# Reordering VectorE and GpSimd work in a conditioned block with Strassen-type products: sums, one normalised tile, statistics, a gather

## The chip, the cores and the metric

The kernel runs on one core of a Trainium2 chip. Its engines each run their own queue of instructions in order: TensorE (PE; its weight loads are listed apart as PEld), VectorE (DVE), ScalarE (ACT), GpSimd (POOL) and SyncE (SP), which issues most DMAs. They wait for one another by semaphores. The metric is device time in microseconds (us): the median of three runs before the change is 456.7 us (455.54 to 456.86).

## The reference

Thirty-two sequences of 128 tokens with 512 features pass through a conditioned block. `t` is one row of conditioning for each sequence, `m` the mask of tokens.

```
emb = silu(t) @ ada_w + ada_b;  shift, scale, gate = split(emb, 3)
norm = where(m, layernorm(x) * (1 + scale) + shift, 0)
ssm  = gelu(norm @ ssm_w1 + b1) @ ssm_w2 + b2  (+ the same with bwd weights)
x    = x + gate * where(m, ssm, 0)
ff   = silu(t) @ ffada_w + ffada_b;  shift2, scale2, gate2 = split(ff, 3)
n2   = layernorm(x) * (1 + scale2) + shift2
h    = gelu(n2 @ ff_w1 + ff_b1)            # 512 -> 1024
out  = x + gate2 * (h @ ff_w2 + ff_b2)     # 1024 -> 512
```

All is float32. In the first half only tokens that the mask keeps are computed. The second half, from `ff` on, is dense over all 4096 tokens and takes most of the time.

## The kernel before

**Opening** (to about 83 us): conditioning rows, the first half on 512 gathered slots of tokens, whose rows go to `x1_rows` in DRAM, and sums of the weights of the feed-forward layer, kept in `t_rows` in DRAM.

**Pairs.** The second half goes in four pairs `p` of two sides; a side is four sequences. For every pair there are two products, each done with seven multiplications of quarter blocks in place of eight (Strassen's scheme in the form with few additions).

*First product* (class `FirstProduct`, L1024): `h` of a pair. It is cut twice: seven *streams* of the outer scheme, in the order 1, 2, 5, 6, 3, 7, 4 (`STREAMS`, L1015), and in each stream seven multiplications P1 to P7. One multiplication is a *phase* (`phase`, L1108), which writes one of the two PSUM banks `e` and `a` of its stream and then starts what the result needs. `window(new, old, fill)` (L1206) interleaves two streams:

```
(new, "P5"), (new, "P1"), (old, "P3"), (old, "P7"),
(new, "P2"), (new, "P6"), (old, "P4"),
```

After phase `n` of window `w` it runs the functions put at `(w, n)` by `put`. The steps that matter here, with their lines:

- `token_sums(j, n)` (L1036): DVE sums of quarters of the tokens, for `j` = 1 to 4 and four blocks `n`: L1046 (into `sx`, read by stream 5), L1050 (into `xn_sy`, read by stream 6), L1053 and L1056 (in place, for streams 7 and 4). Both inputs lie in SBUF. Pair 0 calls them at L1406 to L1426; later pairs inside the windows, their first ones at the end of the pair before.
- `seed` (L1157): once P1 is in `a`, it goes to `e`, on DVE with an earlier result added (L1161; streams 2, 6, 3, 7, 4) or on ACT (L1163). P2 then adds to `e` on PE, so PE waits for the seed.
- P6: DVE L1142 puts `a` plus an earlier sum into `e`; P3 adds to `e` and waits for it. P7: DVE L1147 takes `a` out into `hb`; P4 adds to `a` and waits for it. P4: L1152.
- `with_p5` (L1165, POOL L1168), `after` (POOL L1197) and `late_sum` (POOL L1201) are POOL's sums of 128x512, all in SBUF. `late_gelu` and `release` start ACT's gelu (L1079).

*Second product* (class `SecondProduct`, L1225): steps in `ORDER` (L902), "P1U P5U P1V P5V ...", U and V being two units of columns. `first_block` (DVE L1251) sums parts of `hb` into `s1`, which P5 reads; `seed` (L1239) starts its banks from `fb2` and `fb2_step` on ACT (L1243); L1261, L1268, L1278, L1280, L1326, L1328 and L1334 are its other DVE sums. The end of the first product is woven into it: stream 4's P3, P7 and P4 run between its first steps.

*The next pair's tokens.* `take_first_half` (POOL L885) gathers rows of the first half from `x1_rows` with an indirect DMA, one for each sequence, eight for each pair. `Statistics` (L904) has `one(i)` (DVE bn_stats and its aggregate, L917 and L918) for each tile, and `root` (DVE L922 `ve`, then POOL L923 `rstd`) for a side. `blocks(side, i)` normalises tile `i` (DVE L929) and transposes its 32x32 blocks (L1479). `to_feature_rows` issues 16 DMAs for a side from SP (L956), ACT scales what lands (L939), and `TokenBlocks.one` (L986) makes the sums that the next pair's first phases read. In pair 0 `fw2_of.combine` (L394) also makes sums of the second weights.

**What sets the order.** Everything from the opening on stands in a region of manual scheduling: each engine's queue is in the order in which the Python code issues the instructions. A wait of one instruction holds all behind it on its engine. The DVE queue before, around the first pair's start, is: `sx` blocks 0 and 1, stream 1's P6 (L1142), stream 2's seed, stream 1's P7 (L1147), `sx` blocks 2 and 3, stream 2's P6, the four `xn_sy` blocks, L1053 block 0, `fb2_step`, L1053 block 1, stream 2's P7 (L1147), and so on.

Of the kernel before, what the change touches and what calls it, by code (L numbers as in the profile page):

```python
# [14 lines left out]
ALU = mybir.AluOpType  # L15
# [7 lines left out]
def kernel(  # L23
# [49 lines left out]
    nc = tc.nc  # L73
    B, S, D = x.shape
    P = 128
    assert S == P
    G = 4
# [99 lines left out]
    def group_of_tiles(name):  # L177
        return xnp.tile([P, G, D], F32, tag="xn", name=f"xn_{name}")
# [398 lines left out]
    for key, vec in (("ssm1", ssm_b1), ("bwd1", bwd_b1), ("ff1", ff_b1)):  # L577
        n = vec.shape[0] // P
# [78 lines left out]
    fb2 = const.tile([P, D], F32, name="fb2")  # L657
# [177 lines left out]
    def in_turned_blocks(t):  # L835
        return t.rearrange("p i d -> p (i d)").rearrange("p (k i c) -> p k i c", i=G, c=P)
# [37 lines left out]
    fb2_step = const.tile([P, D // 2], F32, name="fb2_step")  # L874
# [7 lines left out]
    def take_first_half(p, xs, which=range(2 * G)):  # L882
        for i in which:
            b = 2 * p * G + i
            nc.gpsimd.indirect_dma_start(  # L885
                out=xs[i // G][i % G // 2][:, i % 2],
                out_offset=None,
                in_=x1_rows,
                in_offset=bass.IndirectOffsetOnAxis(ap=slot_i[:, b : b + 1], axis=0),
                bounds_check=NS - 1,  # L890
                oob_is_err=False,
            )
# [71 lines left out]
    def new_xT(p, side):  # L964
        return xtp.tile([P, KC, G * S], F32, tag=f"xT{side}", name=f"xT_{p}_{side}")
# [436 lines left out]
    now = FirstProduct(0, of_x[0].cut(), of_w)  # L1402
    now.load_weights(1)
    x_of[1][1] = load_side(1, 1)
    now.load_weights(2)
    for n in range(2):  # L1406
        now.token_sums(1, n)
    now.apart(1)
    now.do(1, "P1")
    now.seed(1)  # L1410
    now.do(2, "P1")
    now.do(1, "P5", "P2", "P6")
    now.do(2, "P5")
    now.seed(2)
    now.do(1, "P3")
    now.with_p5(2, "12")
    now.do(1, "P7")
    now.with_p5(2, "22")
    take_first_half(1, x_of[1], range(G))
    for n in range(2, 4):  # L1420
        now.token_sums(1, n)
    now.do(2, "P2", "P6")
    for n in range(4):
        now.token_sums(2, n)
    now.do(1, "P4")
    now.token_sums(3, 0)  # L1426
    for p in range(NP):
        more_pairs = p + 1 < NP
        xs = x_of[p]
        fills = {}  # L1430

        def put(w, n, f, *args):
            fills.setdefault(w, {}).setdefault(n, []).append(lambda: f(*args))

        if p:
            for n, at in enumerate(((1, 3), (1, 4), (1, 6))):
                put(*at, now.token_sums, 2, 1 + n)
            put(1, 6, now.token_sums, 3, 0)
        for n, at in enumerate(((2, 1), (2, 3), (2, 3))):
            put(*at, now.token_sums, 3, 1 + n)  # L1440
        for n, at in enumerate(((2, 4), (2, 4), (2, 6), (2, 6) if more_pairs else (3, 1))):
            put(*at, now.token_sums, 4, n)
        put(3, 6, now.load_weights, 3)
        if p == 0:
            put(3, 6, load_rows_of_fw2, 0)
            put(6, 2, fw2_of.combine, 0)
            put(6, 5, fw2_of.combine, 1)
        put(4, 6, now.load_weights, 4)
        if p == 0:
            put(4, 6, load_rows_of_fw2, 1)  # L1450
        second = SecondProduct(p, now.h, xs)
        if p == 0:
            put(
                2, 0, nc.vector.tensor_tensor,
                fb2_step, fb2[:, D // 2 :], fb2[:, : D // 2], ALU.subtract,
            )
        put(6, 0, now.late_gelu, "11")
        put(6, 1, second.seed, 0)
        put(6, 3, second.first_block, 0, 0, 2)
        put(6, 6, second.first_block, 0, 2, 4)  # L1460
        put(5, 4, now.late_sum, "11")
        put(6, 4, now.late_gelu, "12")
        put(6, 5, now.late_gelu, "22")
        put(6, 6, now.late_sum, "21")
        if more_pairs:
            x_next = x_of[p + 1]
            stats = [Statistics(x_next[side], f"{p + 1}_{side}") for side in range(2)]
            xn, xT = {}, {}

            def blocks(side, i):  # L1470

                if i == 0:
                    xn[side] = in_turned_blocks(
                        group_of_tiles(f"{p + 1}_0")
                        if side == 0
                        else sp.tile([P, G, D], F32, tag="s12", name=f"xn_{p + 1}_1")
                    )
                t = stats[side].normalised(i, xn[side][:, :, i])
                nc.vector.transpose(t, t)  # L1479

            def to_feature_rows(side, *queues):
                xT[side] = new_xT(p + 1, side)
                turned(xn[side], xT[side], queues)

            if p:
                put(1, 6, take_first_half, p + 1, x_next, range(G))
            put(2, 6, take_first_half, p + 1, x_next, range(G, G + 2))
            put(3, 4, take_first_half, p + 1, x_next, range(G + 2, G + 3))
            put(5, 4, take_first_half, p + 1, x_next, range(G + 3, 2 * G))
            for i, at in enumerate(((3, 1), (3, 3), (3, 4), (3, 6))):  # L1490
                put(*at, stats[0].one, i)
            put(*((3, 6) if p else (5, 4)), stats[0].root)
            for i, at in enumerate(((4, 4), (4, 6), (5, 3), (6, 4))):
                put(*at, stats[1].one, i)
            put(6, 4, stats[1].root)
        for w in range(1 + (p == 0), 7):
            now.window(STREAMS[w], STREAMS[w - 1], fills.get(w, {}))
        second.load_gate(0)
        second.step(0)
        now.late_gelu("21")  # L1500
        if more_pairs:
            for i in range(2):
                blocks(0, i)
        now.do(4, "P3")
        second.seed(1)
        now.do(4, "P7")
        second.first_block(1, 2, 4)
        if more_pairs:
            blocks(0, 2)
        second.step(1, late=True)  # L1510
        now.do(4, "P4")
        if more_pairs:
            blocks(0, 3)
            to_feature_rows(0, nc.sync)
        second.load_gate(1)
        second.first_block(1, 0, 2)
        second.seed_and_second_block(0)
        fill = {5: [lambda: second.third_block(0)], 7: [lambda: second.third_block(1)]}

        def put(step, f, *args):  # L1520
            fill.setdefault(step, []).append(lambda: f(*args))

        if p == 0:
            put(2, fw2_of.combine, 2)
            put(6, fw2_of.combine, 3)
        if more_pairs:

            for i in range(G):
                put(2 + i // 2, blocks, 1, i)
            for k in range(KC):  # L1530
                put(4 + k // 2, lambda k: scaled(2 * (p + 1), xT[0], k), k)
                put(7 + k // 2, lambda k: scaled(2 * (p + 1) + 1, xT[1], k), k)
                if k == 1:
                    put(4, to_feature_rows, 1, nc.sync, nc.sync, nc.sync, nc.scalar)

            def begin(j):
                if j == 1:
                    of_x[p + 1] = TokenBlocks(p + 1, (xT[0], xT[1]))
                of_x[p + 1].one(j)

            put(8, begin, 1)
            put(9, begin, 2)
            put(9, begin, 3)
            put(10, begin, 4)

            def next_product():
                nxt["p"] = FirstProduct(p + 1, of_x[p + 1].cut(), of_w)
                nxt["p"].load_weights(1)

            nxt = {}  # L1550
            put(10, next_product)
            put(11, lambda: nxt["p"].do(1, "P5", "P1"))
            for n in range(4):
                put(11 + n // 2, lambda n: nxt["p"].token_sums(1, n), n)
            put(13, lambda: nxt["p"].token_sums(2, 0))
            if p + 2 < NP:
                x_of[p + 2] = [[], []]
                put(11, lambda: x_of[p + 2][0].extend(load_side(p + 2, 0)))
            put(12, lambda: nxt["p"].do(1, "P2", "P6"))
            put(13, lambda: nxt["p"].load_weights(2))  # L1560
            if p + 2 < NP:
                put(13, lambda: x_of[p + 2][1].extend(load_side(p + 2, 1)))
        for step in range(2, len(ORDER)):
            second.step(step)
            for f in fill.get(step, ()):
                f()
        if more_pairs:
            now = nxt["p"]
# [11 lines left out]
    with tc.If(more > 0):  # L1580
# [11 lines left out]
        with tc.For_i(0, more, 1):  # L1592
# [12 lines left out]
            for half_no, (mod, was, wbs, bias, bcol, func) in enumerate(  # L1605
# [7 lines left out]
                for j, w in enumerate(was):  # L1613
                    n = FF // len(was)
                    nc.sync.dma_start(wa[:, :, ts(j, n)], w.rearrange("(k p) f -> p k f", p=P))
                for j, w in enumerate(wbs):
                    n = HC // len(wbs)
# [73 lines left out]
```

## Time and profile before

One execution was profiled. Its own time is 455.45 us, of which the span from first to last instruction is 453.7 us.

| what | value |
|---|---|
| median of three runs | 456.7 us |
| profiled execution, time / span | 455.45 / 453.7 us |
| mean granted clock of PE | 0.999 |
| busy: PE / DVE / ACT / POOL | 446.6 / 331.7 / 178.0 / 159.8 us |
| share of the last chain: PE / DVE | 92% / 5% |
| instructions: PE / DVE / ACT / POOL | 2151 / 571 / 390 / 154 |
| first product of pair 0 begins; pairs 1, 2, 3 begin | 83.4; 169.4, 260.4, 351.3 us |

A row of a timeline gives the start and the length in us, the engine, the line, the operation, the tile written and the tiles read (numbers of buffers left out), the shape, and how many records were joined. In brackets stands the idle time of the engine ahead of the row and what ended it. A row's length on DVE includes the fill and drain of its pipe: two rows that follow each other directly start 0.60 us apart at 128x512 though each is listed with 0.68. A row with PE's weight loads (PEld) stands 0.22 us ahead of its matmuls as long as PE is not held up.

### The profile page before, as it was taken

How to read it: one execution, taken by the hardware profiler on the slowest of the kernel's cores; microseconds unless marked ns; L12 is line 12 of the kernel's file. 1: busy time of each engine (PE TensorE's matmuls, PEld its weight loads, DVE VectorE, ACT ScalarE, POOL GpSimd, SP SyncE). 2: the span in 40 equal slices, each digit the busy share in tenths (PEclk: the TensorE clock that was granted, in tenths of full speed). 3: DMA queues.
4: the chain of work that ended last, by engine and by line, in shares of the span. 5: the costliest groups of instructions: out<-in, count | busy, mean ns of one | idle time of the engine just before them, and what ended most of it. 6: DMA issues, size and time to landing. Idle time of an engine off the chain costs nothing.

```text
span 453.7 us, 6170 instructions
## 1 busy us (share of the span) xinstructions
PE 446.6 (98%) x2151; PEld 370.4 (82%) x2151; DVE 331.7 (73%) x571; ACT 178.0 (39%) x390; POOL 159.8 (35%) x154
## 2 busy tenths in 40 slices
PE   8999999999999999999999999999999999999996
PEld 3884585688888888888888888888888888888885
DVE  5798797697789759886796498867963995534645
ACT  3124127244642552446425514454355154552000
POOL 4220550089770000797700007977000027560000
PEclk9999999999999999999999999999999999999999
DMA  7999449745518817722187167221872442222023
GB/s 251 379 396 407 150 73 326 279 151 172 189 78 180 114 49 251 249 92 82 66 191 107 56 230 264 95 84 54 202 105 59 157 145 82 81 94 93 0 82 107
DMA packets 82611, 70.57 MB, mean 156 GB/s; under 512 B 63112, under 2 KB 63728, under 8 KB 81554
## 3 DMA queue, kind: packets, MB, share of 16 engines
q1 hardware_dynamic: 67762, 58.28, 40.9%
q0 software_dynamic: 4160, 10.54, 6.9%
q10 hardware_dynamic: 10656, 1.33, 2.1%
q8 instruction: 18, 0.29, 0.2%
q14 instruction: 15, 0.12, 0.1%
HBM read 56.46 MB, written 13.70 MB: 155 GB/s over the span
## 4 chain that ended last, share of the span: by engine, by line
PE 92%; DVE 5%; POOL 1%; issue 1%; ACT 1%; DVEq 0%
PE a_o L1304 23%; PE a_m L1117 18%; PE e_o L1304 18%; PE e_m L1117 14%; PE po_s L221 6%; PE ph_s L204 5%; PE ph_s L673 2%; PE pm_ss L309 1%; PE last L1304 1%; PE pm_f L309 1%; PE a_m_alone L1117 1%; PE pl_s L254 1%; DVE xn_sy L1050 0%; PE part_s L333 0%; DVE e_m L1142 0%
## 5 line engine op out<-in xcount | busy, mean ns | idle before, releaser
L1168 POOL TENSOR_TENSOR ha<-p_m,ha 128x512 f32<-128x512 f32 x20 | 25.8, 1289 | 178.8 <-ACT ha L1175 169.2
L1304 PE MATMUL e_o<-fw,ha 128*128 128x256 f32 x256 | 57.9, 379 | 0.0
L939 ACT ACTIVATE xT<-xT,modT 128x128 f32<-128x128 f32 x112 | 44.1, 480 | 31.6 <-DMA xT<-xn 31.4
L1304 PE MATMUL a_o<-t,hb 128*128 128x256 f32 x240 | 54.1, 379 | 0.0
L1304 PEld LDWEIGHTS e_o<-fw,ha 128*128 128x128 f32 x256 | 48.6, 190 | 6.6
L1304 PEld LDWEIGHTS a_o<-t,hb 128*128 128x128 f32 x240 | 45.6, 190 | 6.2
L1079 ACT ACTIVATE hb<-hb,biasT 128x256 f32<-128x256 f32 x64 | 29.0, 500 | 30.4 <-POOL hb L1201 19.8
L1131 ACT COPY p_m<-e_m 128x512 f32<-128x512 f32 x27 | 15.8, 586 | 47.8 <-PE e_m L1117 43.3
L885 POOL DMA_INDIRECT x<-x_rows,slot_i x24 | 29.2, 1218 | 6.0 <-issue 5.3
L1168 POOL TENSOR_TENSOR hb<-p_m,hb 128x512 f32<-128x512 f32 x20 | 29.6, 1481 | 0.3
L1304 PE MATMUL a_o<-fw,ha 128*128 128x256 f32 x128 | 28.9, 379 | 0.0
L1304 PE MATMUL a_o<-t,s 128*128 128x256 f32 x128 | 28.9, 379 | 0.0
L1304 PE MATMUL e_o<-fw,s 128*128 128x256 f32 x128 | 28.9, 379 | 0.0
L221 PE MATMUL po_s<-w,h_s 128*128 128x512 f32 x64 | 28.4, 594 | 0.0
L1175 ACT COPY ha<-e_m 128x512 f32<-128x512 f32 x32 | 18.5, 578 | 24.9 <-PE e_m L1117 24.6
L1304 PEld LDWEIGHTS a_o<-t,s 128*128 128x128 f32 x128 | 24.3, 190 | 3.3
L1304 PEld LDWEIGHTS a_o<-fw,ha 128*128 128x128 f32 x128 | 24.3, 190 | 3.3
L1304 PEld LDWEIGHTS e_o<-fw,s 128*128 128x128 f32 x128 | 24.3, 190 | 3.3
L1142 DVE TENSOR_TENSOR e_m<-a_m,ha 128x512 f32<-128x512 f32 x20 | 13.9, 696 | 17.0 <-POOL ha L1168 6.6
L1079 ACT ACTIVATE ha<-e_m,biasT 128x256 f32<-128x256 f32 x48 | 20.0, 468 | 14.8 <-PE e_m L1117 12.6
L1117 PE MATMUL a_m<-xT,tw 128*128 128x256 f32 x96 | 24.7, 380 | 0.4 <-DVE hb L1147 0.4
L1117 PE MATMUL e_m<-s,fw 128*128 128x256 f32 x92 | 23.8, 381 | 0.0
(237 smaller groups left out, 892.3 us busy)
## 6 DMA issues: line engine op xcount, KB each, us to landing
tw<-t_rows SPq DMA_DIRECT2D x16, 896.0 KB, 5.3
x<-in_x_dram SPq DMA_DIRECT2D x16, 512.0 KB, 8.8
gate<-gate_rows POOLq DMA_DIRECT2D x8, 1024.0 KB, 5.2
out_dram<-x SPq DMA_DIRECT2D x15, 512.0 KB, 4.9
xT<-xn SPq DMA_DIRECT2D x92, 64.0 KB, 2.4
ada_f<-in_L_cond_ffada_w_dram SPq DMA_DIRECT2D x4, 768.0 KB, 13.2
ada_a<-in_L_cond_ada_w_dram SPq DMA_DIRECT2D x4, 512.0 KB
w<-in_L_cond_ssm_w_dram SPq DMA_DIRECT2D x2, 1024.0 KB, 6.2
```

The lines of the kernel that those rows point to most:

```text
L204: nc.tensor.matmul(ph[:, :n], w[:, k, ts(f, P)], xT[:, k, :], start=(k == 0), stop=(k == KC - 1))
L221: nc.tensor.matmul(po, h[f][:, ts(i, P)], w[:, f, :], start=(f == 0 and seeded is None), stop=(f == HC - 1), skip_group_check=seeded is no ...
L309: nc.tensor.matmul(pm[ts(j, B), : (hi - lo) * P], sT[:, k, :], kinds[:, k, lo:hi, ts(j, P)], start=False, stop=True, skip_group_check=True,)
L885: nc.gpsimd.indirect_dma_start(out=xs[i // G][i % G // 2][:, i % 2], out_offset=None, in_=x1_rows, in_offset=bass.IndirectOffsetOnAxis(ap= ...
L939: nc.scalar.activation(out, src, AF.Identity, bias=shift, scale=scale)
L1079: nc.scalar.activation(dst[:, n], src[:, n], AF.Gelu_apprx_tanh, bias=biasT[:, f : f + 1])
L1117: nc.tensor.matmul(bank[:, ts(n, QT)], self.w_block(j, product)[:, ts(n, P)], self.x_block(j, product), start=(product in ("P1", "P5") and ...
L1131: nc.scalar.copy(p5, e)
L1142: nc.vector.tensor_tensor(e, a, p5, add)
L1168: nc.gpsimd.tensor_tensor(self.place(RESULT[j], c), self.p5[j], other, ALU.add)
L1175: nc.scalar.copy(self.place(RESULT[j], c), src)
L1304: nc.tensor.matmul(part, src[:, k, ts(i, P)], w[product][:, k, :], start=(last and k == 0), stop=True, skip_group_check=True,)
```

## The change

Only the places in the order move; no instruction is added, removed or changed in shape. PE, ACT and SP issue the same instructions in the same order as before.

- Pair 0: all four `sx` blocks and then `fb2_step` stand ahead of stream 1's P6. `xn_sy` block 0 stands between stream 1's P6 and stream 2's seed, block 1 between that seed and stream 1's P7; blocks 2 and 3 stay behind stream 2's P6. On POOL the seventh gather (first row of tile `x_14`) moves from behind stream 6's three sums to ahead of them.
- All pairs: of side 0's statistics, `one(3)` moves from the end of window 3 to window 4 behind stream 3's seed, and from pair 1 on `root` with it (POOL's `rstd` then stands behind stream 3's two L1168 sums). Of side 1's, `one(1)` moves behind stream 7's seed. The root of side 1 moves behind `first_block(0, 2, 4)` on DVE and behind the last L1201 on POOL.
- Pair 0: the second tile to be normalised (`blocks(0, 1)`) moves behind stream 4's P7 (L1147).
- From pair 1 on: `xn_sy` block 0 (a sum for stream 6) moves from the end of the pair before to window 1, behind stream 2's seed.

```diff
-    for n in range(2):
+    for n in range(4):
         now.token_sums(1, n)
+    nc.vector.tensor_tensor(fb2_step, fb2[:, D // 2 :], fb2[:, : D // 2], ALU.subtract)
     now.apart(1)
     now.do(1, "P1")
     now.seed(1)
     now.do(2, "P1")
     now.do(1, "P5", "P2", "P6")
+    now.token_sums(2, 0)
     now.do(2, "P5")
     now.seed(2)
+    now.token_sums(2, 1)
     now.do(1, "P3")
     now.with_p5(2, "12")
     now.do(1, "P7")
     now.with_p5(2, "22")
     take_first_half(1, x_of[1], range(G))
+    now.do(2, "P2", "P6")
     for n in range(2, 4):
-        now.token_sums(1, n)
-    now.do(2, "P2", "P6")
-    for n in range(4):
         now.token_sums(2, n)
     now.do(1, "P4")
...
         if p:
-            for n, at in enumerate(((1, 3), (1, 4), (1, 6))):
-                put(*at, now.token_sums, 2, 1 + n)
+            for n, at in enumerate(((1, 1), (1, 3), (1, 4), (1, 6))):
+                put(*at, now.token_sums, 2, n)
...
-        if p == 0:
-            put(
-                2, 0, nc.vector.tensor_tensor,
-                fb2_step, fb2[:, D // 2 :], fb2[:, : D // 2], ALU.subtract,
-            )
...
-            put(2, 6, take_first_half, p + 1, x_next, range(G, G + 2))
-            put(3, 4, take_first_half, p + 1, x_next, range(G + 2, G + 3))
+            put(2, 6, take_first_half, p + 1, x_next, range(G, G + 2 + (p == 0)))
+            if p:
+                put(3, 4, take_first_half, p + 1, x_next, range(G + 2, G + 3))
             put(5, 4, take_first_half, p + 1, x_next, range(G + 3, 2 * G))
-            for i, at in enumerate(((3, 1), (3, 3), (3, 4), (3, 6))):
+            for i, at in enumerate(((3, 1), (3, 3), (3, 4), (4, 1))):
                 put(*at, stats[0].one, i)
-            put(*((3, 6) if p else (5, 4)), stats[0].root)
-            for i, at in enumerate(((4, 4), (4, 6), (5, 3), (6, 4))):
+            put(*((4, 1) if p else (5, 4)), stats[0].root)
+            for i, at in enumerate(((4, 4), (5, 1), (5, 3), (6, 4))):
                 put(*at, stats[1].one, i)
-            put(6, 4, stats[1].root)
+            put(6, 6, stats[1].root)
...
         if more_pairs:
-            for i in range(2):
+            for i in range(1 + (p > 0)):
                 blocks(0, i)
         now.do(4, "P3")
         second.seed(1)
         now.do(4, "P7")
+        if more_pairs and p == 0:
+            blocks(0, 1)
         second.first_block(1, 2, 4)
...
-            put(13, lambda: nxt["p"].token_sums(2, 0))
```

## The prediction

> **What bounds the kernel now.** I read the share of busy time and the chain first, then TensorE's (PE's) rows in order of time, then VectorE's (DVE's) and GpSimd's (POOL's) rows around every place where PE is late. From the page:
>
> ```profile
> PE 446.6 (98%) x2151; PEld 370.4 (82%) x2151; DVE 331.7 (73%) x571; ACT 178.0 (39%) x390; POOL 159.8 (35%) x154
> PE 92%; DVE 5%; POOL 1%; issue 1%; ACT 1%; DVEq 0%
> ```
>
> PE is the bound; only its gaps can be won. A phase is four matmul records, 0.864 us from its start to the next one's; sixteen are 3.455. PE's timeline (start, length) shows the exceptions:
>
> ```profile
> 97.75 1.03 PE L1117 MATMUL a_m<-sx,tw 128*128 128x256 f32 x4
> 99.00 1.13 PE L1117 MATMUL a_m<-xT,t 128*128 128x256 f32 x4 [0.23 <-DVE hb L1147]
> 99.97 1.03 PE L1117 MATMUL e_m<-xn_sy,tw 128*128 128x256 f32 x4
> ...
> 129.89 3.62 PE L1304 MATMUL e_o<-fw,s 128*128 128x256 f32 x16
> 133.93 1.13 PE L1117 MATMUL a_m<-xT,tw 128*128 128x256 f32 x4 [0.42 <-DVE hb L1147]
> ...
> 207.63 1.13 PE L1117 MATMUL e_m<-xT,tw 128*128 128x256 f32 x4
> ...
> 365.35 1.13 PE L1117 MATMUL e_m<-xT,fw 128*128 128x256 f32 x4
> ```
>
> From 97.75 to 99.00 is 1.25, so 0.39 is lost, and the phase after takes 0.97, another 0.10 that follows each such stop. In this way: stream 2 P4 (99.00) 0.49; stream 5 P3 (101.75) 0.16; stream 6 P2 (103.88) 0.41; stream 4 P4 (133.93) 0.69; stream 7 P2 in pairs 1 and 2 (207.63, 298.58) 0.28 each; stream 2 P2 in pair 3 (365.35) 0.29. Together 2.60 us. All wait for DVE, which is in other work. Outside these places, two more before 90 us and the start and end, PE's rows stand shoulder to shoulder.
>
> Why DVE is late, from its timeline and POOL's:
>
> ```profile
> 92.58 1.48 DVE L1046 TENSOR_TENSOR sx<-s 128x256 f32<-128x256 f32 x1
> ...
> 131.28 1.27 DVE L929 TENSOR_SCALAR xn<-x,mv,rstd 128x512 f32<-128x512 f32 x1
> ...
> 137.37 0.65 DVE L1251 TENSOR_TENSOR s<-hb 128x512 f32<-128x512 f32 x1
> ...
> 201.58 0.69 DVE L1147 TENSOR_TENSOR hb<-a_m,hb 128x512 f32<-128x512 f32 x1 [0.93 <-PE a_m L1117]
> ...
> 216.19 0.30 DVE L922 TENSOR_SCALAR ve<-mv 128x4 f32<-128x4 f32 x1
> ```
>
> ```profile
> 92.08 1.71 POOL L1168 TENSOR_TENSOR hb<-p_m,hb 128x512 f32<-128x512 f32 x1
> ...
> 98.59 1.00 POOL L885 DMA_INDIRECT x<-x_rows,slot_i  x1 [0.31 <-issue]
> 99.89 2.07 POOL L885 DMA_INDIRECT x<-x_rows,slot_i  x1 [0.30 <-issue]
> ...
> 131.00 1.26 POOL L1201 TENSOR_TENSOR hb<-hb 128x512 f32<-128x512 f32 x1
> ...
> 215.17 1.29 POOL L1201 TENSOR_TENSOR ha<-ha 128x512 f32<-128x512 f32 x1 [2.77 <-ACT ha L1175]
> ```
>
> A DVE sum of two SBUF tiles costs 0.41 (256 wide) or 0.68 alone, but 1.48 at 92.58: it ends 0.27 after POOL's 92.08 sum does (93.79). The normalised tile takes 1.27 in place of 0.53 and ends 0.29 after POOL's 131.00. The small ve takes 0.30 at 216.19 and ends at 216.49, POOL's at 216.46; without POOL such a tile takes 0.17. So these operations and POOL's sums take turns, one whole instruction at a time. Sums that read PSUM (L1142, L1147, L1152, L1161) and bn_stats keep 0.6 to 0.7 beside POOL.
>
> **The change part by part** (PE, ACT and SP keep their order; only DVE's and POOL's change).
>
> *First pair's sums.* Sums (1,2), (1,3) and fb2_step (0.60 + 0.34 + 0.34 from start to start) move to 86.15, where DVE idles 2.02 until 88.25: they end at 87.43. fb is issued at 77.4; with the 8.8 of other x loads it lands by 86.9, with 2.4 (the shortest kind) by 80.5: in time at both ends. Block (2,0) goes into the 0.71 idle before 89.66, (2,1) into the 0.68 before 91.04. So the pair 91.65 to 93.99 vanishes, 2.34 with its contention, and stream 2's P7 result (L1147) starts when PE allows, 96.02 + 1.13 (that lag stands in pair 1, 188.42 to 189.55) = 97.15, not 98.27. From there DVE has the sequence that it has in pair 1, where stream 6's seed starts 4.94 after that L1147 (194.49) and PE is never late. Gain: 0.49 + 0.16 + 0.41 = 1.06, all of it.
>
> *The seventh gather* now stands ahead of stream 6's sums on POOL; what queues behind it is L1168 twice, L1197, and through it stream 3's seed on DVE. POOL's sum ends at 93.4 (no contention), then seven gathers of at least 1.00 with 0.30 between: 102.7 if nothing disturbs; the six of before took 2.63 more in all, those of pair 1 1.23. DVE's sequence is now pair 1's, so I take 1.23: 103.9; ends 102.7 and 105.4. The Trainium skill ("SBUF — State Buffer", Who interferes with whom) says that a two-input DVE sum contends only with a GpSimd instruction that reads SBUF, not with one that only writes; read so, a gather's descriptors should not suffer, and 102.7 would be the time. The 2.07 row beside plain sums stands against that reading, and I do not use it. Stream 3's seed needs POOL three sums later (3.73), 107.6; PE frees it at 106.39 (107.44 less the gain) + 1.16 (as 107.44 to 108.60) = 107.55; the seed takes 0.76 with its signal, and PE's weight load is due at 108.76 (110.03 less 1.05, loads running 0.22 ahead). Slack 0.4: cost 0, up to 1.0 at the late end.
>
> *Statistics behind seeds.* In pairs 1 and 2 stream 7's seed goes ahead of bn_stats: at 206.07 instead of 206.89, so 0.28 per pair is won, with the 0.03 stop at 205.69. The bn_stats fall into DVE's idle 0.68 (209.92). But ve of side 0 now stands after stream 3's seed (199.95) and a bn_stats: 201.5. POOL, no longer in the root, runs L1168 twice from 200.06 to 202.55, and ve waits for the second: 202.58. Behind it stands L1147 of stream 6 P7 (201.58 before): 202.55 to 203.24, so PE's P4 starts at 203.30, not 203.11: 0.19 + 0.10 lost. Net per pair 0.31 − 0.29 = +0.02. If ve is not held, +0.31; ends −0.1 and +0.31. I take the held one, because three ve beside POOL sums end 0.03 after them.
>
> *One normalised tile, and the second root.* In pair 0, tile 1 moves behind stream 4's L1147, so P4 no longer waits 0.69. What is late next is unit V's P5 of the second product at 138.35: it needs L1251 (137.37 to 138.02), due for the weight load at 138.13. PE has no more than 0.05 there. DVE has no idle time from 126.19 (which follows PE through ACT and POOL, so 125.14 now) to 137.37. After L1251 (129.02 at its end) 6.57 of work is left (7.30 less the 0.73 of the tile's wait). ve stands there now; POOL's last sum, no longer behind the root, takes its turn at 129.09 and ends at 130.25, so ve and all behind it start at 130.25. L1251 then starts at 130.25 + 6.57 = 136.82, ends 137.47, PE follows at 137.53 instead of 138.35: 0.82 less 0.10 for the stop. So pair 0 keeps 0.72 of 1.06 + 0.69 = 1.75, as DVE sets that point. Ends: 0.72 − 0.25 if one more POOL operation comes between; 1.75 if DVE gets its turn first. In pairs 1 and 2 ve does the same, and L1201 runs ahead of the root: the wait of 0.84 at 224.50 goes, tile 0 waits about as long again; L1147 ends near 224.9, when the weight load is due (224.94). Cost 0 to 0.1.
>
> *Pair 3.* Stream 2's seed goes ahead of one sum (0.60): 0.29 won; if pair 2's tiles are 0.34 later, 0.2. I take 0.25.
>
> Sum: 0.72 + 0.02 + 0.02 + 0.25 = 1.0 us. The profiled execution took 455.45 (span 453.7), so 454.45; it lies 1.25 under the median of the runs, 456.7, so 455.7 for a median. About 0.3% (1.37 us) is what a measurement of this kernel can tell from no change.
>
> **The rivals.**
> *Everything comes through* (faster): DVE is not held where I hold it, and all 2.60 plus the two 0.03 are won: 454.1. For it: the waits named are exactly those that the order removes. Against it: the 1.27 and 1.48 rows, and 0.05 of slack at 138.13.
> *GpSimd becomes late*: seven gathers at the old mean, (104.09 − 93.94) / 6 = 1.69 each, end at 105.4; stream 3's seed starts at 109.1, PE gets it at 109.9 instead of 108.98: 0.9 + 0.10. The gain is gone: 456.7. It decides from 104.3 on. Against: pair 1's mean is 1.46.
> *The tiles are held in every pair* (slower): ve waits for L1168, tile 0 for L1201, tile 1 for the root, 1.2 + 1.26 + 1.05 in place of the 0.96 of before. Tile 1 is then 2.6 late; L1147 of stream 4 P4 has 1.23 of slack (223.65 + 0.06 to 224.94), so PE loses 1.4 + 0.10 in pairs 1 and 2, and pair 3's gain goes with the later transposes: −3.0 + 0.7 = 2.3 slower, 459.0. It decides from tile 1 being 1.2 late on. Against: the root beside tile 0 at 130.07 left it at 0.53.
>
> **How the numbers follow.** Forecast 0.42, everything 0.34, GpSimd late 0.13, tiles held 0.11. The forecast's own range, by its ends, is 454.8 to 456.6, and a third of it (0.14) lies more than 0.3% under 456.7. Faster 0.34 + 0.14 = 0.48; slower 0.10 of the last; the rest 0.42. The range 453.9 to 457.1 takes in the first three cases with their ends and leaves out the last.
>
> **What would show it.** Right: no stop of PE from 97 to 108 and at stream 4 P4 (or under 0.2), a stop of 0.6 to 0.9 at unit V's P5 in pair 0, one of 0.2 to 0.3 at stream 6 P4 in pairs 1 and 2, ve at 1.0 us or more there, seven gathers ending near 103.9. Wrong: PE tight at those P5 and P4 rows (ve short), or a wait of stream 3's seed for L1197, or DVE's tiles over 1.2 in pairs 1 and 2 with PE waiting for them.

## The result, and the profile after

The changed kernel takes 454.84 us (median of 13 runs, 453.79 to 455.84) beside 456.02 us for the kernel before (13 runs, 455.04 to 456.87). The ratio is 0.9971, its 95% interval 0.9959 to 0.9982: 1.18 us less by the medians, about 0.3%. The forecast was 1.0 us less. The interval spans 0.8 to 1.9 us, so which terms of the forecast came true is read from PE's stops below, not from the times.

The profiled execution of the changed kernel took 454.99 us with a span of 453.3 us, so one execution against one other shows 0.46 us only. The page has the same bound as before:

```profile
PE 446.3 (98%) x2151; PEld 370.5 (82%) x2151; DVE 334.2 (74%) x571; ACT 178.4 (39%) x390; POOL 159.0 (35%) x154
...
PE 94%; DVE 3%; POOL 1%; ACT 1%; issue 1%
```

DVE's share of the chain that ended last went from 5% to 3%, and its busy time rose by 2.5 us with the same instructions, since a held instruction counts as busy: the six rows of ve take 4.3 us more in all, those of L1046 1.4 less. PE's timeline of the changed kernel at the places shown before, and where new stops came:

```profile
97.80 1.03 PE L1117 MATMUL a_m<-sx,tw 128*128 128x256 f32 x4
98.67 1.03 PE L1117 MATMUL a_m<-xT,t 128*128 128x256 f32 x4
99.53 1.03 PE L1117 MATMUL e_m<-xn_sy,tw 128*128 128x256 f32 x4
...
132.34 1.03 PE L1117 MATMUL a_m<-xT,tw 128*128 128x256 f32 x4
133.20 3.62 PE L1304 MATMUL a_o<-fw,ha 128*128 128x256 f32 x16
137.44 3.72 PE L1304 MATMUL e_o<-fw,s 128*128 128x256 f32 x16 [0.62 <-DVE s L1251]
...
202.44 1.13 PE L1117 MATMUL a_m<-xn_sy,tw 128*128 128x256 f32 x4
...
293.38 1.13 PE L1117 MATMUL a_m<-xn_sy,tw 128*128 128x256 f32 x4
...
368.90 1.13 PE L1117 MATMUL e_m<-s,fw 128*128 128x256 f32 x4
```

From 97.80 to 99.53 the phases follow each other every 0.86 us; the stops of 0.49, 0.16 and 0.41 are gone, and so is that of 0.69 at stream 4 P4 (132.34). The sixteen records from 133.20 on take 3.455, so unit V's P5 is due at 136.66; it comes at 137.44, 0.79 late, and 0.10 follows. The rows of 1.13 in place of 1.03 mark the other phases after a stop. Why DVE is late there, from its and POOL's timelines:

```profile
129.06 1.23 DVE L922 TENSOR_SCALAR ve<-mv 128x4 f32<-128x4 f32 x1
130.20 0.54 DVE L929 TENSOR_SCALAR xn<-x,mv,rstd 128x512 f32<-128x512 f32 x1
...
136.73 0.65 DVE L1251 TENSOR_TENSOR s<-hb 128x512 f32<-128x512 f32 x1
...
291.64 1.09 DVE L922 TENSOR_SCALAR ve<-mv 128x4 f32<-128x4 f32 x1
292.65 0.68 DVE L1147 TENSOR_TENSOR hb<-a_m,hb 128x512 f32<-128x512 f32 x1
```

```profile
128.55 1.71 POOL L1201 TENSOR_TENSOR hb<-hb 128x512 f32<-128x512 f32 x1
...
291.42 1.27 POOL L1168 TENSOR_TENSOR hb<-p_m,hb 128x512 f32<-128x512 f32 x1
```

Four elements for each partition (ve) take 1.23 and 1.09 us: ve ends 0.03 to 0.04 after POOL's sum (130.26, 292.69), and what stands behind it starts then.

PE's stops that wait for DVE or ACT, from 95 us to the end, in us (the extra pitch of the phase plus the 0.10 after it; small ones under 0.06 counted in):

| place | before | after | after, second profile |
|---|---|---|---|
| pair 0, streams 2, 5, 6 (97 to 104) | 1.06 | 0 | 0 |
| pair 0, stream 4 P4 / unit V's P5 | 0.69 / 0 | 0 / 0.89 | 0 / 0.91 |
| pair 1 | 0.31 | 0.29 | 0.29 |
| pair 2 | 0.30 | 0.30 | 0.28 |
| pair 3 | 0.30 | 0.36 | 0.20 |
| sum | 2.66 | 1.84 | 1.67 |

The sum falls by 0.82, not by the 0.46 of the two execution times. The rest: the first product began 0.06 later (an opening that the change does not touch), and in the profile after PE stops 0.30 more at 385.64 for a transfer of weights, which is taken up at the end.

### The profile page after: what moved, and what is told of

Same layout as the page of the kernel before. It is cut to its first block, busy times and chain, and to the rows that moved or that the text cites. A ratio compares the mean times of both kernels' runs of the same rounds, so it can differ in the third digit from the quotient of the medians.

```text
span 453.3 us, 6170 instructions
## 1 busy us (share of the span) xinstructions
PE 446.3 (98%) x2151; PEld 370.5 (82%) x2151; DVE 334.2 (74%) x571; ACT 178.4 (39%) x390; POOL 159.0 (35%) x154
## 4 chain that ended last, share of the span: by engine, by line
PE 94%; DVE 3%; POOL 1%; ACT 1%; issue 1%
PE a_o L1304 22%; PE a_m L1117 20%; PE e_o L1304 18%; PE e_m L1117 15%; PE po_s L221 6%; PE ph_s L204 5%; PE ph_s L673 2%; PE pm_ss L309 1%; PE last L1304 1%; PE a_m_alone L1117 1%; PE pm_f L309 1%; DVE s L1251 1%; PE part_s L333 0%; PE pl_s L254 0%; DVE xn L929 0%
## 5 line engine op out<-in xcount | busy, mean ns | idle before, releaser
L1168 POOL TENSOR_TENSOR ha<-p_m,ha 128x512 f32<-128x512 f32 x20 | 26.3, 1313 | 178.6 <-ACT ha L1175 168.8
L885 POOL DMA_INDIRECT x<-x_rows,slot_i x24 | 27.2, 1135 | 6.2 <-issue 5.4
L1168 POOL TENSOR_TENSOR hb<-p_m,hb 128x512 f32<-128x512 f32 x20 | 29.2, 1460 | 0.3
L1142 DVE TENSOR_TENSOR e_m<-a_m,ha 128x512 f32<-128x512 f32 x20 | 14.0, 698 | 17.0 <-POOL ha L1168 7.6
```

The lines of the kernel that those rows point to most:

```text
L885: nc.gpsimd.indirect_dma_start(out=xs[i // G][i % G // 2][:, i % 2], out_offset=None, in_=x1_rows, in_offset=bass.IndirectOffsetOnAxis(ap= ...
L1142: nc.vector.tensor_tensor(e, a, p5, add)
L1168: nc.gpsimd.tensor_tensor(self.place(RESULT[j], c), self.p5[j], other, ALU.add)
```

## The experiments

All times below stand beside runs of the kernel before on the same chip and in the same session.

The stops are counted from 95 us on, as above; an expectation that says 3.18 counts the 0.52 before that, which stays. The ratio is not the quotient of the two medians: for side 1's root back it is 0.9968 where the medians give 0.9951, for the first sum of stream 6 back 0.9956 where they give 0.9967. So what sets apart two rows that differ by 0.2% or less is the stops, not the times.

| kernel | median | before | ratio, 95% interval | stops by DVE or ACT |
|---|---|---|---|---|
| sums alone (on before) | 456.01 | 456.75 | 0.9991, 0.9976 to 1.0006 | 2.65 |
| gather back (on after) | 456.39 | 455.99 | 1.0004, 0.9990 to 1.0019 | 2.59 |
| root of side 1 back (on after) | 454.51 | 456.75 | 0.9968, 0.9948 to 0.9988 | 0.88 |
| tile 1 alone (on before) | 455.89 | 456.02 | 0.9995, 0.9980 to 1.0011 | 2.73 |
| root of side 0 later (on after) | 456.48 | 456.75 | 1.0002, 0.9987 to 1.0017 | 3.18 |
| first sum of stream 6 back (on after) | 455.25 | 456.75 | 0.9956, 0.9931 to 0.9981 | 1.92 |
| changed kernel again | 454.54 | 456.02 | 0.9969, 0.9954 to 0.9984 | 1.67 |
| rearranged order | 454.01 | 455.99 | 0.9946, 0.9920 to 0.9972 | 0.22 |
| rearranged order again | 453.61 | 456.02 | 0.9936, 0.9913 to 0.9959 | 0.56 |

### The first pair's sums alone, and the gather back

The first is the kernel before with this alone (and the old places of these calls taken out):

```diff
-    for n in range(2):
+    for n in range(4):
         now.token_sums(1, n)
+    nc.vector.tensor_tensor(fb2_step, fb2[:, D // 2 :], fb2[:, : D // 2], ALU.subtract)
...
+    now.token_sums(2, 0)
     now.do(2, "P5")
     now.seed(2)
+    now.token_sums(2, 1)
```

> The kernel before with the first part of the change alone: the first pair's sums and the bias step placed early, everything else as before. My theory: the three stops of TensorE at 99.00, 101.75 and 103.88 (1.06 us together) go and nothing comes in their place, because VectorE's work from 125 us on follows TensorE; the stop of 0.69 at stream 4 P4 and those of the later pairs stay. TensorE's stops add up to 2.1 in place of 3.18; time 1.06 us under before, ratio 0.9977. Rival (what is won early is given back later in the pair, because gathers or loads set the pace there): ratio 0.999 or more, with a new stop of 0.5 or more before 140 us.

Measured: 456.01 us, ratio 0.9991; stops 2.65, as before. The three stops of 1.06 went, and one of 0.93 + 0.10 came at stream 6 P2. The theory missed. The rival's signs came true (0.999 or more, a new stop over 0.5 before 140 us), but not its reason, that gathers or loads set the pace: the six gathers end 2.2 us earlier than before, at 101.88, POOL's first sum of stream 6 starts at 101.89 in place of 104.11, and DVE's last sum for stream 6, at 102.02, is held until it is done (1.49 in place of 0.41). So the seventh gather was the next thing to test:

```diff
-            put(2, 6, take_first_half, p + 1, x_next, range(G, G + 2 + (p == 0)))
-            if p:
+            put(2, 6, take_first_half, p + 1, x_next, range(G, G + 2))
+            if True:
                 put(3, 4, take_first_half, p + 1, x_next, range(G + 2, G + 3))
```

> The changed kernel with the seventh gather back behind GpSimd's sums of stream 6, as before the change. Theory A (from the run with the sums alone: without the seventh gather GpSimd's first sum of stream 6 starts at 101.9, just as VectorE's last sum of stream 6 starts at 102.0, and that sum waits for a whole GpSimd instruction): the 256-wide sum takes 1.5 in place of 0.42, the seed of stream 6 is 1.0 late, TensorE stops 0.93 + 0.10 at stream 6 P2 near 104; ratio to before about 0.9995. Theory B (the gather's place costs and saves nothing, as my prediction had it): no stop between 89 and 136 us, time that of the changed kernel, ratio 0.997.

Measured: 456.39 us, ratio 1.0004: undoing this one move costs the whole gain. DVE, POOL and PE with the gather back:

```profile
103.92 1.50 DVE L1056 TENSOR_TENSOR s<-s,xn_sy 128x256 f32<-128x256 f32 x1
105.34 0.69 DVE L1161 TENSOR_TENSOR e_m<-a_m,ha 128x512 f32<-128x512 f32 x1
```

```profile
102.78 1.00 POOL L885 DMA_INDIRECT x<-x_rows,slot_i  x1 [0.30 <-issue]
103.80 1.34 POOL L1168 TENSOR_TENSOR ha<-p_m,ha 128x512 f32<-128x512 f32 x1
```

```profile
106.08 1.13 PE L1117 MATMUL e_m<-xn_sy,tw 128*128 128x256 f32 x4 [0.77 <-DVE e_m L1161]
```

The changed kernel at the same place (2.2 us earlier, as its opening ended earlier):

```profile
101.75 0.42 DVE L1056 TENSOR_TENSOR s<-s,xn_sy 128x256 f32<-128x256 f32 x1
...
102.09 0.69 DVE L1161 TENSOR_TENSOR e_m<-a_m,ha 128x512 f32<-128x512 f32 x1
```

```profile
101.92 1.13 POOL L885 DMA_INDIRECT x<-x_rows,slot_i  x1 [0.30 <-issue]
103.07 1.28 POOL L1168 TENSOR_TENSOR ha<-p_m,ha 128x512 f32<-128x512 f32 x1
```

With the gather ahead, POOL's sum starts 1.3 us after DVE's last sum, which takes 0.42; without it the two start 0.12 apart and DVE's takes 1.50. Theory A holds. The gather is no filler: it keeps POOL off the tiles until DVE is through. In the kernel before two gathers took 2.07 and 1.83, so that POOL's sum came only at 104.11, after that DVE sum too; why they took so long is shown at the end.

### Side 1's root back, and tile 1 alone

```diff
-            put(6, 6, stats[1].root)
+            put(6, 4, stats[1].root)
```

> The changed kernel with the root of side 1 back at its old place, right behind the last statistics (all pairs). My theory (the small ve operation stands where GpSimd is summing and waits for it, and everything behind it is late): in the first pair ve takes 0.3 us near 123.5, tile 0 starts at 129.06 and takes 0.54, stream 4's result follows about 1.1 us earlier than in the changed kernel, tile 1 is held until GpSimd's moved sum ends (about 131), and the stop of 0.89 us at unit V's P5 goes; stops in pairs 1 and 2 as in the changed kernel or 0.05 smaller. Time 0.9 us under the changed kernel, ratio to before about 0.995. Rival (VectorE simply has too much work between 125 and 137 us, wherever ve stands): the stop shrinks by ve's own 0.3 at most, to 0.6, ratio about 0.9965.

Measured: 454.51 us, ratio 0.9968. DVE, then PE and ACT, with the root back:

```profile
123.30 0.30 DVE L922 TENSOR_SCALAR ve<-mv 128x4 f32<-128x4 f32 x1
...
135.68 0.65 DVE L1251 TENSOR_TENSOR s<-hb 128x512 f32<-128x512 f32 x1
```

```profile
132.10 1.03 PE L1117 MATMUL a_m<-xT,tw 128*128 128x256 f32 x4
133.24 3.72 PE L1304 MATMUL a_o<-fw,ha 128*128 128x256 f32 x16
136.80 3.40 PE L1304 MATMUL e_o<-fw,s 128*128 128x256 f32 x15
```

```profile
131.07 0.91 ACT L1079 ACTIVATE hb<-hb,biasT 128x256 f32<-128x256 f32 x2 [3.98 <-POOL hb L1201]
...
132.60 0.59 ACT L1243 COPY a_o<-fb 128x512 f32<-128x512 f32 x1
```

L1251 comes at 135.68 in place of 136.73, and unit V's P5 follows without a stop: the hold of ve was the cause of the 0.89, not the amount of DVE's work. The time does not decide between theory (0.995) and rival (0.9965): the interval holds both, and this profile stops 0.98 near 385 us for a reason taken up at the end. And a stop of 0.39 that was not expected comes at 133.24. With POOL's power of the root ahead of the last L1201, that sum ends 0.77 later though PE is 0.24 ahead in this execution, ACT's late activation with it (131.07 against 130.29 in the changed kernel), and the bias seed behind it on ACT (132.60 + 0.59) makes PE wait. So the new place of the root has two sides: ve on DVE is 0.89 worse there, the power on POOL 0.39 better. Tile 1 moved alone shows the second side by itself:

```diff
         if more_pairs:
-            for i in range(2):
+            for i in range(1 + (p > 0)):
                 blocks(0, i)
...
         now.do(4, "P7")
+        if more_pairs and p == 0:
+            blocks(0, 1)
```

> The kernel before with tile 1 of the first pair alone moved behind stream 4's P7 result. My theory, mended by the run with side 1's root at its old place: the stop of 0.69 at stream 4 P4 goes, unit V's P5 is not late, but the late activation behind GpSimd's last sum keeps ScalarE's bias seed where it was, so that TensorE stops 0.4 to 0.5 at the phase after; kept 0.2 to 0.3 us, ratio 0.9995. By the step of my prediction alone (tile 1 and nothing else late): stop at unit V's P5 of 0 to 0.1 and all of 0.69 kept, ratio 0.9985.

Measured: 455.89 us, ratio 0.9995. The stop of 0.69 goes, P5 is not late, and 0.39 is lost at the phase behind P4:

```profile
132.97 1.03 PE L1117 MATMUL a_m<-xT,tw 128*128 128x256 f32 x4
134.12 3.72 PE L1304 MATMUL a_o<-fw,ha 128*128 128x256 f32 x16
```

132.97 + 0.86 is 133.83; PE starts at 134.12, when ACT's seed (133.48 + 0.59) has ended. The moved tile keeps 0.30 of its 0.69, as the mended theory said. (All stops of this run add to 2.73 because pair 3 lost 0.65 in its profile, at a long lag as shown below.)

### Side 0's root one step later

```diff
-            put(*((4, 1) if p else (5, 4)), stats[0].root)
+            put(*((4, 3) if p else (5, 4)), stats[0].root)
```

> The changed kernel with the root of side 0 in pairs 1 and 2 one step later: ve behind stream 6's P7 result in place of ahead of it. My theory: that result starts at 291.8 in place of 292.65 (as soon as TensorE gives it), the stops of 0.23 and 0.24 at stream 6 P4 go, ve takes 0.3 to 0.5 behind it, nothing else is late: 0.47 us under the changed kernel, ratio to before about 0.996. Rival (the statistics ahead of it are what makes the result late): the stops stay at 0.15 or more and the time is that of the changed kernel.

Measured: 456.48 us, ratio 1.0002; the theory's forecast missed. DVE, POOL and PE of this kernel in pair 1:

```profile
200.52 0.69 DVE L1147 TENSOR_TENSOR hb<-a_m,hb 128x512 f32<-128x512 f32 x1
201.13 2.85 DVE L922 TENSOR_SCALAR ve<-mv 128x4 f32<-128x4 f32 x1
```

```profile
200.24 1.27 POOL L1168 TENSOR_TENSOR hb<-p_m,hb 128x512 f32<-128x512 f32 x1
201.47 1.26 POOL L1197 TENSOR_TENSOR ha<-ha 128x512 f32<-128x512 f32 x1
202.69 1.25 POOL L1197 TENSOR_TENSOR hb<-hb 128x512 f32<-128x512 f32 x1
```

```profile
205.47 1.13 PE L1117 MATMUL e_m<-s,fw 128*128 128x256 f32 x4 [0.67 <-DVE e_m L1142]
```

The first half came true: L1147 starts at 200.52 as soon as PE allows, and the stop at stream 6 P4 is gone in both pairs. But ve takes 2.85, not 0.3 to 0.5: it is held through the rest of one POOL sum and through two whole ones, until 203.98, when POOL has a gap. What stands behind ve is then late, and stream 3's phase behind its P6 stops 0.94 in pair 1 and 0.92 in pair 2. So an operation of DVE does not always get its turn between two of POOL's.

### The moved sum of stream 6 in pair 3

```diff
-            for n, at in enumerate(((1, 1), (1, 3), (1, 4), (1, 6))):
-                put(*at, now.token_sums, 2, n)
+            for n, at in enumerate(((1, 3), (1, 4), (1, 6))):
+                put(*at, now.token_sums, 2, 1 + n)
...
+            put(13, lambda: nxt["p"].token_sums(2, 0))
```

> The changed kernel with the first sum of stream 6 of the next pair back at its old place, ahead of stream 2's seed. Theory A (in pair 3 VectorE's whole run of work hangs on the turned tiles, which came only 0.41 us earlier while TensorE came 0.83 earlier): the seed ends 0.6 later than in the changed kernel, the stop at stream 2 P2 grows from 0.12 to 0.6 to 0.7 and the stop of 0.24 at 368.9 goes, so pair 3 loses 0.3 more than the changed kernel; ratio to before about 0.9978. Theory B (the moved sum runs beside GpSimd's first sum of stream 2, and this collision makes what follows late): the stop at stream 2 P2 is the old 0.29 and the one at 368.9 goes; pair 3 loses as much as or less than in the changed kernel, ratio 0.997 or less.

Measured: 455.25 us, ratio 0.9956, whose interval (0.9931 to 0.9981) holds the forecasts of both. Pair 3 stops 0.47 at stream 2 P2 alone, between A (0.6 to 0.7) and B (0.29). What decides shows when all profiles are laid side by side. From 348 us DVE works without a break, and its start hangs on ACT's scaled tiles:

```profile
348.22 1.22 DVE L986 TENSOR_TENSOR s<-xT 128x1024 f32<-128x1024 f32 x1 [6.44 <-ACT xT L939]
```

That is the changed kernel; its PE began the block of that time at 347.06, so DVE's start lags by 1.16. In the kernel before it is 348.63 - 347.89 = 0.74:

```profile
348.63 1.23 DVE L986 TENSOR_TENSOR s<-xT 128x1024 f32<-128x1024 f32 x1 [6.03 <-ACT xT L939]
```

The lag and the stops of pair 3 in every profile:

| order | lag: stops of pair 3 (us) |
|---|---|
| old (sum ahead of the seed) | 0.74: 0.30 (before); 0.77: 0.33 (sums alone); 0.92: 0.47 (sum back); 1.09: 0.65 (tile 1 alone) |
| new (seed first) | 0.72: 0 (root 1 back); 0.83: 0.03 (rearranged); 0.84: 0.05 (gather back); 0.99: 0.20 (after again); 1.15: 0.33 (root 0 later); 1.16: 0.36 (after); 1.22: 0.42 (rearranged again); 1.35: 0.55 (two sums added); 1.51: 0.71 (two fills added) |

In both rows the stops grow by as much as the lag: they are the lag less 0.44 in the old order, less 0.80 in the new. So at the same lag the new order loses 0.36 less (or all, where the old loses less than that). A holds as to the mechanism (the run hangs on the turned tiles), and missed by the lag of its execution.

But the lag is not the same before and after. From the last tile of side 0 on, SP issues the transfers of both sides one behind the other (from 318.6 to 340.1 us in the changed kernel; a few go by ACT), and that tile comes nearer to PE's block there: L929 at 317.26 is 29.80 ahead of 347.06, in the kernel before 317.85 is 30.04 ahead of 347.89. With side 1's root back it is 30.05 (316.18 and 346.23). So the root's new place should take back 0.24 of the 0.36. The lags agree on average, but they scatter widely between executions: 1.13 (0.84 to 1.51) over seven profiles that have the tiles of the changed kernel, 0.83 (0.72 to 1.09) over four that have them as before; the rearranged order, which has that tile 30.27 ahead, lags 0.83 and 1.22. The scatter is not DVE's: from side 1's last transposed tile to PE's block it is 20.36 or 20.37 in all thirteen profiles. It lies in the issues and transfers between; what makes it was not tried.

### Sums and fills of GpSimd put beside DVE's sums

Two operations were added to the changed kernel on POOL where DVE makes the first pair's sums; their result is not used. `late` is a tile in SBUF that the opening leaves (`t_s` in POOL's row).

```diff
+    spare = gp.tile([P, 512], F32, tag="spare", name="spare")
+    for _ in range(2):
+        nc.gpsimd.tensor_tensor(spare, late, late, ALU.add)
```

> The changed kernel with two sums of SBUF tiles (128x512) added on GpSimd, which the first pair's sums on VectorE (85.0 to 87.5, 0.60 apart) then meet; their result is not used. Taking turns: each GpSimd sum (1.27 alone) holds one VectorE sum for its length, so one or two of VectorE's sums take 1.3 to 1.9, the row ends at 89.5 to 90 in place of 87.5, and TensorE, which had 0.7 of slack there, stops 1.2 to 1.8. No contention: 0.60 apart as before, no stop.

> The same with two fills of the tile by GpSimd (which write SBUF and read nothing) in place of the two sums, behind a sum of one column that sets their start. If only a GpSimd instruction that reads SBUF holds VectorE: VectorE's sums stay 0.60 apart and TensorE does not stop, as in the changed kernel. If writing holds it too: one or two VectorE sums take over 1.0 and TensorE stops 0.5 or more near 89.

One execution of each. DVE, POOL and PE with the two sums:

```profile
85.31 2.98 DVE L1046 TENSOR_TENSOR sx<-xT 128x512 f32<-128x512 f32 x2
```

```profile
85.02 2.71 POOL L1409 TENSOR_TENSOR spare<-t_s 128x512 f32<-128x512 f32 x2 [21.41 <-DMA x<-in_x_dram]
```

```profile
89.62 1.13 PE L1117 MATMUL e_m<-s,fw 128*128 128x256 f32 x4 [0.85 <-DVE e_m L1142]
```

DVE and POOL with the two fills:

```profile
87.49 1.29 DVE L1046 TENSOR_TENSOR sx<-xT 128x512 f32<-128x512 f32 x2
```

```profile
87.68 1.11 POOL L1410 MEMSET spare<- 128x512 f32 x2
```

Beside sums DVE's pair takes 2.98 in place of 1.29, each of the two about 1.5, and PE stops 1.12 where the changed kernel stops 0.27: 0.86 more, somewhat under the 1.2 to 1.8 expected. Beside fills the pair takes 1.29, and PE stops no more than in the changed kernel. So POOL's writing alone does not hold these sums; what the sums on POOL do besides is to read SBUF. The Trainium skill ("SBUF — State Buffer", Who interferes with whom) says just that: a DVE instruction with two inputs in SBUF contends with a GpSimd instruction that reads SBUF, and not with one that only writes it. These two runs agree with it.

### A rearranged order

For side 1, ve is set apart from the power: ve right behind its statistics, the power where the change has it. In pair 0, tile 0 goes behind stream 4's P7 too; from pair 1 on, side 0's fourth statistics and root go back ahead of stream 3's seed.

```diff
+        def power(self):
+            nc.gpsimd.tensor_tensor(self.rstd, self.ve, half[:, :G], ALU.pow)
...
-            nc.gpsimd.tensor_tensor(self.rstd, ve, half[:, :G], ALU.pow)
+            self.ve = ve
...
-            for i, at in enumerate(((3, 1), (3, 3), (3, 4), (4, 1))):
+            for i, at in enumerate(((3, 1), (3, 3), (3, 4), (3, 6) if p else (4, 1))):
...
-            put(*((4, 1) if p else (5, 4)), stats[0].root)
+            put(*((3, 6) if p else (5, 4)), stats[0].root)
+            put(*((3, 6) if p else (5, 4)), stats[0].power)
...
-            put(6, 6, stats[1].root)
+            put(6, 4, stats[1].root)
+            put(6, 6, stats[1].power)
...
-            for i in range(1 + (p > 0)):
+            for i in range(2 * (p > 0)):
...
         if more_pairs and p == 0:
+            blocks(0, 0)
             blocks(0, 1)
```

> The changed kernel with ve and the power after it set apart: ve of side 1 right behind its statistics (VectorE idle, GpSimd not yet at its next sum), the power on GpSimd behind its last sum as in the changed kernel; in the first pair tile 0 behind stream 4's P7 result; in pairs 1 and 2 side 0's fourth statistics and root back ahead of stream 3's seed. My theory: ve takes 0.3 at each place, the stops of 0.89 (unit V's P5), of 0.23 and 0.24 (stream 6 P4) and the two of 0.05 go, none of 0.39 comes at 133 because the late activation follows GpSimd's last sum without the power between; tiles of side 0 in pairs 1 and 2 come 1.2 earlier and the stops of 0.36 in pair 3 shrink to 0.2 or less. TensorE's stops after 95 us add up to 0.2 to 0.5 in place of 1.85; 1.4 to 1.6 us under the changed kernel, ratio to before about 0.994. Rival (what VectorE must do between 125 and 137 is too much in any order): a stop of 0.5 or more stays at unit V's P5, ratio 0.996.

> The changed kernel once more, beside the next one on the same chip, to set the two against each other. TensorE's stops after 95 us by VectorE 1.85 us in all at the same places as before; ratio to before 0.9965 to 0.998. A stop of 0 to 1.1 where stream 3's phase of the last pair waits for its weights (near 385) may be there or not, by how late they land.

> The same order as in best1 (ve apart from the power, tile 0 behind the P7 result, side 0's root ahead of the seed). My theory: stops of TensorE after 95 us by VectorE 0.2 us, so 1.6 us less than the changed kernel beside it; ratio to before 0.994 to 0.995, 0.9965 of the changed kernel. Rival: the gain of the first run was the chip's, and the two are within 0.5 us.

Measured: 0.9946 (0.9920 to 0.9972), and in a second session 0.9936 (0.9913 to 0.9959) beside 0.9969 (0.9954 to 0.9984) for the changed kernel: 453.61 against 454.54 us there. The two intervals still touch, so that it beats the changed kernel rests on the stops as well: 0.22 and 0.56 in all, 0.42 of the latter in pair 3 at a lag of 1.22. DVE and PE of the first of these profiles:

```profile
123.78 0.30 DVE L922 TENSOR_SCALAR ve<-mv 128x4 f32<-128x4 f32 x1
...
129.40 0.69 DVE L1147 TENSOR_TENSOR hb<-a_m,hb 128x512 f32<-128x512 f32 x1
130.01 0.79 DVE L929 TENSOR_SCALAR xn<-x,mv,rstd 128x512 f32<-128x512 f32 x1
```

```profile
133.45 3.62 PE L1304 MATMUL a_o<-fw,ha 128*128 128x256 f32 x16
136.90 3.72 PE L1304 MATMUL e_o<-fw,s 128*128 128x256 f32 x16
```

P7's result reads PSUM and takes 0.69 beside POOL's last sum; the tile that would be held stands behind it and is held for only 0.26. PE's two blocks start 3.45 apart, and 0.10 is lost inside the second (3.72 in place of 3.62). The gain over the changed kernel is 0.93 us in the session that ran both, between the theory's 1.6 and the rival's 0.5; the stops there differ by 1.1 (1.67 less 0.56), less than the 1.6 because of the lag in pair 3.

## Why the prediction was right

It forecast 455.7 from a median of 456.7; the runs gave 454.84 from 456.02. The gain of 1.0 stands against 1.18, and against 0.82 and 0.99 by the stops of two profiles of the changed kernel. The waits that it named are the ones that changed, but part of the agreement is luck: two terms were off in opposite ways, and the largest one holds only because of a move that was counted as worth nothing. By its steps:

- **First pair's sums, "Gain: 1.06, all of it".** The size came true, but its reason did not carry it. "From there DVE has the sequence that it has in pair 1, ... and PE is never late" left out what DVE's earlier place does to POOL: its gathers get shorter, and its next sum comes just when DVE's last sum does. With the sums alone 1.03 of the 1.06 stays lost.
- **The seventh gather, "cost 0, up to 1.0 at the late end".** This step failed. It asked only what the gather makes late, and not what would start in its place. The move is worth 1.03 (gather back). The time of the gathers was off too: the seven ended at 103.05, not at 103.9. That this is near the 102.7 of the reading by the Trainium skill ("SBUF — State Buffer", Who interferes with whom), in which sums do not delay a gather's descriptors, is chance. 102.7 counts seven pauses of 0.30 where seven gathers have six between them; undisturbed they would have ended near 102.4. And the sums do delay gathers, as the rows at the end show: the prediction was right not to use that reading, and took the delay too long (1.23 where it was 0.66).
- **Statistics, +0.02 for each of pairs 1 and 2.** Right in both halves: the old stops of 0.28 go, and ve, held behind L1168, makes stream 6 P4 late by 0.23 and 0.24 where 0.29 was said.
- **Tile 1 and side 1's root, "pair 0 keeps 0.72 of 1.75".** Right: ve held until 130.29 (said: 130.25), L1251 at 136.73 (136.82), P5 at 137.44 (137.53), kept 0.86 where 0.72 was said. Not seen: POOL's last sum, freed by the root's move, also feeds ACT, and without this PE would stop 0.39 at the phase behind P4. The step costed the root's move as a loss alone.
- **Pair 3, 0.25.** Too large. The move of the seed is worth 0.36 at an equal lag, but the later tiles, which the step named and let take 0.04 off, should take back 0.24. That would leave 0.12; the two profiles of the changed kernel show -0.06 and +0.10, and the scatter of the lag is larger than either.
- **The rivals.** "Everything comes through" was wrong for this order and right for another: the rearranged one ends at 0.22 to 0.56 of stops. GpSimd was not late. "The tiles are held in every pair" set in by half: in pair 2 ve took 1.24 (0.30 before) and tile 0 1.57 (1.49 before), but tile 1 was not held (0.52), and PE lost only 0.05 there.
- **The mechanism, "take turns, one whole instruction at a time".** Shown by the two sums against the two fills. "Turns" is too kind: ve once waited through the rest of one sum of POOL's and two whole ones.

## What to carry to other kernels

In these traces a VectorE sum of two SBUF tiles, a normalised tile or the small ve beside a GpSimd sum is priced by when that sum ends (once, by when a row of three ended), not by its own size; bn_stats and sums that read PSUM are not. So put the small one where GpSimd has nothing to read, and one that reads PSUM beside the sum. When a move brings one engine forward, look for what the other now meets; an instruction that seems to be filler (the gather) may be what keeps them apart. Such a move can also change how long the other engine's work takes: here the gathers became 2.1 us shorter in all because they met other sums. And a root, or any step issued on two engines, has two places to choose: here one engine wanted it early and the other late, and setting them apart kept both.

## What the runs showed that was not expected

- **A transfer of weights that lands late, by chance.** In pair 3 stream 3's phase waits for its weights near 385 us. It is due 5.85 us after SP begins to issue their load. In thirteen profiles the stop is between 0 and 1.14 us (before 0, after 0.30, again 0.28, sums alone 1.14), and no order of DVE or POOL goes with it. PE with the longest:

```profile
387.56 1.10 PE L1117 MATMUL e_m<-s,tw 128*128 128x256 f32 x4 [0.90 <-DMA tw<-t_rows]
```

  In all profiles the fifteenth of the load's sixteen last packets lands 3.8 to 4.5 us after the issue and the sixteenth at 5.1 to 6.3; the stop grows with that one, from 0 at 5.2. One packet of 16 KB of instructions runs among the load's packets (2.1 us in sums alone, 0.9 in the kernel before). That it is what delays the last one was not tried, and its length alone does not tell: with the gather back it took 2.0, and there was no stop. With the two fills added PE also stopped 0.92 at 120.39 for a load of such weights.
- **A gather's time.** Near 100 us a gather took 2.07 before and 1.28 after. DVE's rows that it meets, in the kernel before (the gather's own row, at 99.89, stands in the prediction):

```profile
99.81 0.67 DVE L1056 TENSOR_TENSOR s<-s,xn_sy 128x512 f32<-128x512 f32 x1
100.41 0.68 DVE L1056 TENSOR_TENSOR xT<-xT,xn_sy 128x512 f32<-128x512 f32 x1
```

  DVE's and POOL's in the changed kernel:

```profile
98.75 0.68 DVE L1056 TENSOR_TENSOR s<-s,xn_sy 128x512 f32<-128x512 f32 x1
```

```profile
99.03 1.28 POOL L885 DMA_INDIRECT x<-x_rows,slot_i  x1 [0.30 <-issue]
```

  The first gather ends at 101.96, 0.95 after DVE went on from these two sums to L1142 (101.01); the second at 100.31, 0.95 after DVE went on from its sum (99.36). One that meets a sum that reads PSUM takes 1.00 (98.59, beside L1147 at 98.27). So a gather that starts while DVE sums two SBUF tiles is held until that sum is through (one that starts within 0.02 us of the sum goes first: 190.78 in the kernel before, 1.00). Tile 1 alone, with DVE's old order there, has 2.06 and 1.83 again; the eleven profiles with the sums placed early have no gather over 1.29 in that stretch. Whether it is the reading of `slot_i` or the writing of descriptors that is held, no run tells.
- **Held through more than one.** ve waited 2.85 us in pair 1 and 2.83 in pair 2 of one kernel, through two whole sums of POOL's, while in pair 2 of the changed kernel it came in between two sums that followed each other as closely (310.93 and 310.89). In the same way the gather at 99.89 waited through two sums of DVE's, the one at 99.03 through one. What decides stays open.
